# Four blocks of gated cross-attention and feed-forward layers: instruction order, the engine of two products and the queue of two transfers

## The chip, the cores and the metric

The kernel runs on one core of one Trainium2 chip. The metric is the time of one execution on the device in microseconds (us). The core has five engines, each of which works off its own instructions in order: TensorE (PE in the profile; its weight loads are PEld), VectorE (DVE), ScalarE (ACT), GpSimd (POOL) and SyncE (SP), which here only issues DMA transfers. An instruction that must wait for another engine or a transfer holds up everything behind it on its own engine.

## The reference

The input is x (32 sequences of 64 tokens, 256 features), a context of the same shape, and two gates of four numbers each. Eight layers follow one another, each of the form x = x + tanh(gate) * layer(layernorm(x), ...). The first three matter here:

```python
x = x + jnp.tanh(g_xattn[0]) * _L0_xattn_ref(32, 64, 256, w, u, _layernorm(x), ctx_2048)   # a decaying weighted mean along the sequence
x = x + jnp.tanh(g_ffn[0]) * _L0_ffn_ref(_layernorm(x), Wg, Wu, Wd, Wr, Ag, Bg, ...)       # experts
x = x + jnp.tanh(g_xattn[1]) * _L1_xattn_ref(_layernorm(x), ctx_2048)                      # convolution along the tokens
```

The first is a recurrence over the 64 tokens with running maxima, its keys being the normalised x and its values the context. In the second, every token is routed to the two best of eight experts. All experts share gate, up and down weights (704 hidden features) and differ by low-rank additions; for each of the two choices the hidden vector is silu(gate) * up. 704 is five times 128 and a remainder of 64. The third is a grouped convolution whose weights are the context. After them come a ternary-weight feed-forward layer, an 8-bit attention, a second ternary one, an attention with rotary positions, and a feed-forward layer with a Hadamard transform.

## The kernel before

The 2048 tokens lie in SBUF as 16 tiles of 128 tokens (c.x) for the whole run. The layers are Python generators, block0 to block7. The driver, program, interleaves them: it calls block1 step by step and, between its steps, as many steps of block0 as a formula allows; later in block1 it calls block2's first steps. Block 0 and block 1 go through the tokens in five chunks of 2, 2, 4, 4 and 4 tiles (CHUNKS), so that the first two chunks have 256 columns and the others 512.

The order in which the program is written is not the order in which an engine gets its instructions. Up to the end of block 3, a planner orders each engine's instructions by modelled times: what its model takes as ready early may go ahead of instructions written before it, and among those that are ready the earlier written one goes first. keep_in_program_order(ins) ties an instruction behind the one written last before it on its engine; it adds no wait for another engine.

The steps that the prediction speaks of:

- Layer norm. _mean (L107) takes a tile's statistics on VectorE (bn_stats, L110; bn_aggr, L113), and _inverse computes 1/sqrt(variance + eps) by a guess from the bits (L124, L92) and three Newton steps of three instructions (L96, L97, L98) on one to four numbers per partition. _stats does this for several tiles; with here=True it ties each bn_stats as above. _norm (L167) applies the result to a tile (xn), and _turned (L181) has TensorE transpose four tiles into PSUM (pt).
- Block 0 (L236 to L326). Per chunk, ScalarE copies the transposed, normalised x into kp (L317), VectorE runs a scan for the maxima (o, L270) and takes a difference (d, L271); exponentials on ScalarE, products on GpSimd, further scans and reciprocals on VectorE follow. w0s is prepared on VectorE at L255. The tanh of the eight gates (L326, in place in c.gate) is written after some steps of the first chunk.
- Block 1 (L333 to L558). head(i0, n) normalises and transposes a chunk (xf, L402 and L403), routes it (route, L363 to L390), spreads the routing over the ranks (ex on GpSimd L411, mt) and makes the low-rank inputs z (pz on TensorE L423, zg and zu on VectorE L426 and their sums on GpSimd L428). The chunk's body then does, for each 128 hidden features f, three gated steps (gated): shared weights alone (TensorE, L462), then the addition of one choice and of the other (L465). Each is followed by silu on ScalarE (sg, L468) and the product h on VectorE (L469), whose reading frees the PSUM bank. The three steps of an f are interleaved with those of the next ones (range(NF + 2)), 15 gated steps in all. The remainder of 64 features comes at the chunk's end (L484 to L501): both choices lie side by side in the partitions, gb and ub are copied from PSUM by ScalarE, and the two products ht[:, 1] = silu(gb) * ub (L491) and ht[:, 0] = silu(gs) * us (L501) are taken. TensorE then runs the down projections (pa L509 and L524, po L515, L532 and, at the next chunk's start, L537); zs is scaled on VectorE (L527, L529) and x updated (L542). The next chunk's head is run ahead, step by step, in the last third of a chunk.
- Block 2 (L565 to L663). Its weights, the context in another layout (c.wb, loaded at L1772 once block 0 has ended), come in two parts, and GpSimd adds their sum as a third part in four instructions of 512 columns (L593). window clears a padded buffer xw (L573). take(xw, q) normalises four tiles, q = 0 to 3, copies the transposed result into xw (L582 to L585) and adds a third part on GpSimd (L587). take 0 and take 1 are written during block 1's last chunk, after its gated steps 6, 8, 10 and 12; the convolution's matmuls (pc, L610) follow block 1.
- Transfers. SyncE issues, in this order, x and wu, the context of the first two chunks (ctx) and x of the second, the two gates (L1794, L1795), constants (con, L1796) and block 1's weights in two halves (wa, L1767 and L1768).

Of the kernel before, what the change touches and what calls it, by code (L numbers as in the profile page):

```python
# [22 lines left out]
ALU = mybir.AluOpType  # L23
# [3 lines left out]
P = 128  # L27
# [79 lines left out]
def _mean(c, pool, mv, i, here=False):  # L107

    st = pool.tile([P, 6], F32, tag="ln_st", name="ln_st", bufs=4)
    ins = c.nc.vector.bn_stats(st, c.x[:, i, :])  # L110
    if here:
        c.tc.keep_in_program_order(ins)
    c.nc.vector.bn_aggr(mv, st)  # L113


def _inverse(c, pool, mv, tag, bufs=1):

    return [r for r in _inverse_slowly(c, pool, mv, tag, bufs)][-1]
# [9 lines left out]
def _stats(c, pool, i0=0, n=NT, bufs=1, here=False):  # L128

    mv = pool.tile([P, max(n, 4), 2], F32, tag="ln_mv", name="ln_mv", bufs=bufs)[:, :n]  # L130
    for j in range(n):
        _mean(c, pool, mv[:, j, :], i0 + j, here)
    return mv, _inverse(c, pool, mv, "ln", bufs), i0
# [37 lines left out]
def _normT(c, pool, ps, ln, g, tag="ps"):  # L171

    return _turned(c, [_norm(c, pool, ln, 4 * g + q) for q in range(4)], ps, tag)
# [17 lines left out]
def _add_gatedT(c, src, hf, q, gate):  # L191

    _add_tilesT(c, src, hf, 4 * q, 4, gate)
# [138 lines left out]
def block1(c):  # L332
# [5 lines left out]
    nc = c.nc  # L338
# [11 lines left out]
    with ExitStack() as es:  # L350
        sm = es.enter_context(c.tc.tile_pool(name="sm1", bufs=1))
# [84 lines left out]
        for t, (i0, n) in enumerate(CHUNKS):  # L436
# [5 lines left out]
            def ahead():  # L442

                nonlocal step
                step += 1
                if nxt and step > STEPS - 8:
                    next(nxt, None)
# [3 lines left out]
            ht = hp.tile([P, 2, 512], F32, tag="ht", name="ht")[:, :, :N]  # L451
# [33 lines left out]
            gb, ub, gs, us = (full(hp, tag, tag) for tag in ("gb", "ub", "gs", "us"))  # L485
            sg = full(tp, "sg", "sg")
# [1 line left out]
                nc.scalar.copy(gb[s * S : (s + 1) * S], pg[:S])  # L488
                nc.scalar.copy(ub[s * S : (s + 1) * S], pg[S:])
            nc.scalar.activation(sg, gb, AF.Silu)  # L490
            nc.gpsimd.tensor_tensor(ht[:, 1, :], sg, ub, ALU.mult)  # L491
            ahead()
            yield
            pg, pu = full(ps, "ps", "pgs"), full(ps, "ps", "pus")
# [3 lines left out]
            nc.vector.tensor_tensor(gs, pg, gb, ALU.add)  # L498
            nc.scalar.activation(gs, gs, AF.Silu)
            nc.vector.tensor_tensor(us, pu, ub, ALU.add)  # L500
            nc.gpsimd.tensor_tensor(ht[:, 0, :], gs, us, ALU.mult)  # L501
            ahead()
            yield
            ahead()
# [52 lines left out]
def block2(c, begin):  # L557

    nc = c.nc
    w = c.wb[:, : 3 * LAGS * P].rearrange("p (k m g o) -> p k m g o", k=3, m=LAGS, g=2)  # L565
    Z = LAGS - 1
    with ExitStack() as es:
        sm = es.enter_context(c.tc.tile_pool(name="sm2", bufs=1, side="right"))

        def window(pool):  # L570

            xw = pool.tile([P, 3, 2, 16, Z + 32], F32, tag="xw", name="xw", bufs=1)
            nc.gpsimd.memset(xw.rearrange("p k h b s -> p (k h b) s")[:, :, 0:Z], 0.0)  # L573
            return xw

        def take(xw, q):

            ln = _stats(c, sm, 4 * q, 4)
            yield
            seqs = slice(8 * (q % 2), 8 * (q % 2) + 8)  # L580
            lo, hi = (pt.rearrange("p (b s r) -> p r b s", s=32, r=2) for pt in _normT(c, sm, c.aux, ln, q, "a"))
            nc.scalar.copy(xw[:, 0, 0, seqs, Z:], lo[:, 0])  # L582
            nc.vector.tensor_copy(xw[:, 1, 0, seqs, Z:], lo[:, 1])
            nc.scalar.copy(xw[:S, 0:2, 1, seqs, Z:], hi[S:])
            nc.vector.tensor_copy(xw[S:, 0:2, 1, seqs, Z:], hi[:S])  # L585
            for h in range(2):
                nc.gpsimd.tensor_tensor(xw[:, 2, h, seqs, Z:], xw[:, 0, h, seqs, Z:], xw[:, 1, h, seqs, Z:], ALU.add)  # L587
            yield

        n = LAGS * P // 4  # L590
        for j in range(4):
            at = [c.wb[:, (4 * k + j) * n : (4 * k + j + 1) * n] for k in range(3)]
            nc.gpsimd.tensor_tensor(at[2], at[0], at[1], ALU.add)  # L593
        xw = window(sm)
        for q in range(2):
            yield from take(xw, q)
        third = begin()
        tn = es.enter_context(c.tc.tile_pool(name="tn2", bufs=2, side="right"))
        ps = es.enter_context(c.tc.tile_pool(name="ps2", bufs=6, space=PSUM))
        fifths = weights5(c, tn)  # L600
        next(fifths)
        xws = [xw, window(tn)]
        casts, waiting, nth = [], [], 0

        def products(xw, k, pcs, lags):
            for m in lags:
                for h in range(2):
                    for a in range(2):
                        rows, to = slice(a * S, (a + 1) * S), slice((a ^ h) * S, ((a ^ h) + 1) * S)
                        nc.tensor.matmul(  # L610
                            pcs[h][to], w[rows, k, m, h, :], xw[rows, k, h, :, Z - m : Z - m + 32], start=m == 0, stop=m == Z
                        )

        def results(k, pcs, kept):

            for h in range(2):
                pv = pcs[h].rearrange("p (b s) -> p b s", s=32)
                if k == 1:
                    p1 = tn.tile([P, 16, 33], F32, tag=f"p1{h}", name=f"p1{h}", bufs=1)
                    yT = tn.tile([P, 1024], F32, tag=f"yT{h}", name=f"yT{h}", bufs=1)  # L620
                    nc.gpsimd.memset(p1[:, :, 0:1], 0.0)
                    nc.scalar.copy(p1[:, :, 1:], pv)
                    kept.append((p1, yT))
                    continue
                p1, yT = kept[h]
                to = yT.rearrange("p (b s r) -> p b s r", s=32, r=2)
                if k == 0:
                    nc.vector.tensor_tensor(to[:, :, :, 0], pv, p1[:, :, :32], ALU.add)
                    nc.vector.tensor_tensor(p1[:, :, 1:], pv, p1[:, :, 1:], ALU.add)
                else:  # L630
                    nc.vector.tensor_tensor(to[:, :, :, 1], pv, p1[:, :, 1:], ALU.subtract)

        slot = 0
        for n in range(2):
            kept = []
            for k in (1, 0, 2):
                pcs = [ps.tile([P, 512], F32, tag="ps", name="pc") for _ in range(2)]
                for part in range(2):

                    for z in casts:  # L640
                        ternary3(c, tn, *z)
                    casts = []
                    for _ in range((1 + (slot % 4 == 0)) if slot else 0):
                        if nth < 12:
                            casts.append(magnitudes3(c, tn, nth))
                            nth += 1
                    next(fifths, None)
                    products(xws[n], k, pcs, range(8 * part, 8 * part + 8))
                    for j in range(2):
                        if waiting:  # L650
                            yT, m, h, q = waiting.pop(0)
                            _add_gatedT(c, yT[:, q * 512 : (q + 1) * 512], h, 2 * m + q, c.gate[:, 1:2])
                    if part:
                        results(k, pcs, kept)
                    elif n == 0 and k in (1, 0):
                        for _ in take(xws[1], 3 - k):
                            pass
                    if slot == 9:
                        next(third)
                    slot += 1  # L660
            waiting = [(kept[h][1], n, h, q) for q in range(2) for h in range(2)]
        for z in casts:
            ternary3(c, tn, *z)  # L663
        for yT, m, h, q in waiting:
            _add_gatedT(c, yT[:, q * 512 : (q + 1) * 512], h, 2 * m + q, c.gate[:, 1:2])
    yield third
# [5 lines left out]
def magnitudes3(c, pool, n):  # L672

    wb = pool.tile([P, 512], BF16, tag="t_wb", name="t_wb", bufs=4)
    ab = pool.tile([P, 512], BF16, tag="t_ab", name="t_ab", bufs=4)
    c.nc.gpsimd.tensor_copy(wb, c.wa[:, n * 512 : (n + 1) * 512])
    c.nc.scalar.activation(ab, wb, AF.Abs)
    return n, wb, ab
# [1061 lines left out]
def program(tc, a, out):  # L1740
    nc = tc.nc
    with ExitStack() as es:
        one = es.enter_context(tc.tile_pool(name="one", bufs=1))
        c = SimpleNamespace(nc=nc, tc=tc)
# [42 lines left out]
        c.aux = es.enter_context(tc.tile_pool(name="aux", bufs=2, space=PSUM))  # L1787


        first, second = block0(c), block1(c)  # L1790
        next(first)
        early, conv_w = ExitStack(), ExitStack()
        c.wts = early.enter_context(tc.tile_pool(name="wts0", bufs=1))
        nc.sync.dma_start(c.gate[:, 0:4], a["g_xattn"].to_broadcast([P, 4]))  # L1794
        nc.sync.dma_start(c.gate[:, 4:8], a["g_ffn"].to_broadcast([P, 4]))  # L1795
        nc.sync.dma_start(c.con, a["con"])  # L1796
        load_wa("l0f", L0F_N)
        pieces, conv = 0, None
# [12 lines left out]
        with ExitStack() as w3s:  # L1811
            for k, _ in enumerate(second):
# [9 lines left out]
                at = k - STEPS * (len(CHUNKS) - 1)  # L1822
# [178 lines left out]
```

## Time and profile before

| | |
|---|---|
| median of 3 runs | 1333.27 us (1330.69 to 1333.59) |
| profiled execution | 1334.85 us, its span 1333.1 us |
| TensorE busy | 1199.2 us (90%) |
| VectorE, ScalarE, GpSimd busy | 905.1, 618.0, 456.1 us |
| 0 to 40 us: TensorE busy | 9.5 us |
| 40 to 365 us (block 1, with most of block 0): TensorE busy | 296.4 of 325 us |
| 365 to 560 us: TensorE busy | 183.4 of 195 us |

Three views of the profile are used. The page gives busy times and the chain of work that ended last, traced back from the last instruction. Busy time by stretches gives, for each stretch, its length, then busy time and instruction count of PE, PEld, DVE, ACT and POOL, then the clock granted to TensorE (1.00 is full speed), the busy share of the DMA engines and GB/s. The instructions in order of time give start, time, engine, line, operation, output and inputs and count; consecutive ones of a group are merged, so the time is that of the group, and the bracket at the end is the engine's idle time before it and what ended that. Times of operations with several entries in flight overlap a little.

### The profile page before, as it was taken

To read this page: it belongs to the slowest core of one execution; us is meant where nothing else is said; L and a number is where in the kernel's file an instruction comes from. 1 tells how busy PE (TensorE), PEld (TensorE's weight loads), DVE (VectorE), ACT (ScalarE), POOL (GpSimd) and SP (SyncE) were. 2 spreads that over 40 slices of the span, in tenths; PEclk is the share of its full clock that TensorE was granted. 3 is DMA by queue.
4 is the path that set the end of the run, shared out by engine and by line. 5 is a ranking of instruction groups with operands and counts; after the bars stand their busy time and mean duration, and the time that the engine had idled before them with its cause. 6 is when DMAs were issued, how large, how long until landed. Compare 5 with 4: busy or idle time off the path is not lost.

```text
span 1333.1 us, 21452 instructions
## 1 busy us (share of the span) xinstructions
PE 1199.2 (90%) x8342; PEld 724.3 (54%) x8342; DVE 905.1 (68%) x2195; ACT 618.0 (46%) x1046; POOL 456.1 (34%) x479
## 2 busy tenths in 40 slices
PE   0788899999999989988899976899999999999999
PEld 0666345454533367765666642455555555555665
DVE  6588867554348898768999996587787877532111
ACT  2553634322231145657899971455555555511100
POOL 3333606120123233335777775123225335000000
PEclk9899999989999999989999997799999999999999
DMA  6000000100052120000000010100000000000000
GB/s 216 21 1 16 0 0 1 63 1 0 8 213 97 33 103 1 1 0 2 2 2 2 2 64 1 60 37 1 2 2 1 2 2 1 1 8 8 16 16 16
DMA packets 10294, 34.14 MB, mean 26 GB/s; under 512 B 1360, under 2 KB 5968, under 8 KB 8528
## 3 DMA queue, kind: packets, MB, share of 16 engines
q1 hardware_dynamic: 10192, 32.76, 6.9%
q8 instruction: 66, 1.08, 0.4%
q14 instruction: 36, 0.29, 0.1%
HBM read 30.66 MB, written 2.10 MB: 25 GB/s over the span
## 4 chain that ended last, share of the span: by engine, by line
PE 56%; DVE 28%; POOL 5%; ACT 4%; issue 4%; DMA 2%; SPq 0%; DVEq 0%; POOLq 0%; ACTq 0%
PE pw L1563 6%; PE po L1586 5%; PE pp L1573 4%; PE po L1735 4%; PE pu L1725 4%; PE pg L1725 4%; PE pc L610 3%; PE pu L462 2%; PE pg L462 2%; PE pu L465 2%; PE pa L509 2%; PE po L515 2%; PE pg L465 2%; DVE xn L167 2%; DMA w<-in_l2f 1%
## 5 line engine op out<-in xcount | busy, mean ns | idle before, releaser
L1579 DVE TENSOR_REDUCE mx<-pp 128x4 f32<-128x1024 f32 x128 | 155.9, 1218 | 42.3 <-PE pp L1573 41.8
L1565 ACT ACTIVATE e<-pw 128x1024 f32<-128x1024 f32 x128 | 130.9, 1025 | 115.0 <-PE pw L1563 68.5
L1563 PE MATMUL pw<-qs,kb 32*128 32x256 f32 x1024 | 147.1, 408 | 7.5 <-DVE qs L1550 4.5
L1573 PE MATMUL pp<-kb,q 32*128 32x512 f32 x512 | 148.8, 665 | 4.8 <-POOL q L1534 4.0
L1563 PEld LDWEIGHTS pw<-qs,kb 32*128 32x128 f32 x1024 | 88.5, 187 | 52.3 <-issue 29.4
L468 ACT ACTIVATE sg<-pg 128x512 f32<-128x512 f32 (+1 forms) x75 | 37.8, 512 | 117.1 <-PE pg L462 51.6
L610 PE MATMUL pc<-xw,wb 64*64 64x512 f32 x768 | 90.0, 600 | 0.2 <-DVE x L542 0.2
L1728 DVE TENSOR_TENSOR h<-pu,sg 128x512 f32<-128x512 f32 x32 | 22.1, 692 | 80.8 <-PE pu L1725 80.8
L1727 ACT ACTIVATE sg<-pg 128x512 f32<-128x512 f32 x32 | 19.1, 597 | 122.8 <-PE pg L1725 122.7
L469 DVE TENSOR_TENSOR h<-pu,sg 128x512 f32<-128x512 f32 (+1 forms) x75 | 42.5, 573 | 49.1 <-PE pu L462 30.4
L1528 POOL TENSOR_TENSOR k<-t,t 128x512 f32<-128x512 f32 x16 | 20.3, 1268 | 148.4 <-DVE t L1513 148.4
L1586 PE MATMUL po<-e,va 128*32 128x256 f32 x1024 | 69.0, 387 | 1.8 <-ACT e L1565 1.8
L768 POOL TENSOR_TENSOR acc<-acc,sq 128x512 f32<-128x512 f32 x28 | 39.0, 1392 | 65.1 <-ACT sq L767 63.6
L1725 PE MATMUL pg<-xf,wa 128*128 128x512 f32 x128 | 60.3, 592 | 0.0
L1725 PE MATMUL pu<-xf,wa 128*128 128x512 f32 x128 | 60.3, 592 | 0.0
L610 PEld LDWEIGHTS pc<-xw,wb 64*64 64x64 f32 x768 | 29.9, 134 | 53.9 <-issue 53.2
L1735 PE MATMUL po<-hb,h 128*128 128x256 f32 x256 | 55.9, 379 | 0.0
L1735 PEld LDWEIGHTS po<-hb,h 128*128 128x128 f32 x256 | 48.6, 190 | 8.3 <-issue 1.9
L110 DVE BATCH_NORM_STATS2 ln_st<-x 128x6 f32<-128x256 f32 x112 | 44.1, 408 | 10.9 <-POOL x L1615 7.2
L1586 PEld LDWEIGHTS po<-e,va 128*32 128x32 f32 x1024 | 26.9, 109 | 44.3 <-issue 17.5
L1513 DVE SCALAR_TENSOR_TENSOR t<-pp,wb,con 128x512 f32<-128x512 f32 x64 | 45.0, 745 | 8.7 <-PE pp L1506 8.7
L1531 POOL TENSOR_SCALAR kb<-k,con 128x512 f32<-128x512 f32 x32 | 49.8, 1569 | 1.6
(342 smaller groups left out, 2946.8 us busy)
## 6 DMA issues: line engine op xcount, KB each, us to landing
w<-in_l2f SPq DMA_DIRECT2D x12, 512.0 KB, 3.9
wa<-in_l0f SPq DMA_DIRECT2D x2, 1828.0 KB, 13.0
wa<-in_l1f SPq DMA_DIRECT2D x2, 1536.0 KB, 9.4
wa<-in_l3f SPq DMA_DIRECT2D x2, 1536.0 KB, 8.0
wb<-in_conv SPq DMA_DIRECT2D x1, 2048.0 KB, 7.4
ctx<-in_ctxT SPq DMA_DIRECT2D x2, 1024.0 KB, 6.0
ctx<-in_ctxN SPq DMA_DIRECT2D x2, 1024.0 KB, 6.3
out<-x SPq DMA_DIRECT2D x16, 128.0 KB, 1.7
```

Of the source, the lines that this page charges most:

```text
L462: nc.tensor.matmul(p, wt[:, k, fc], xf[:, k, :N], start=k == 0, stop=False, skip_group_check=True)
L465: nc.tensor.matmul(p, wt[:, fc], z[m, s][:, :N], start=False, stop=s == 1, skip_group_check=True)
L610: nc.tensor.matmul(pcs[h][to], w[rows, k, m, h, :], xw[rows, k, h, :, Z - m : Z - m + 32], start=m == 0, stop=m == Z)
L1513: nc.vector.scalar_tensor_tensor(t[r], pp[:, :, r, :], bias[:, n, r : r + 1], f, ALU.add, ALU.mult)
L1531: nc.gpsimd.tensor_scalar(kb[:, :, h, :], k, odd[:, h : h + 1], None, ALU.mult)
L1563: nc.tensor.matmul(pw[:, jj, k, :], w.k[rows, h, k * P : (k + 1) * P], w.qs[rows, :], start=True, stop=True)
L1565: nc.scalar.activation(e, pw, AF.Exp, scale=scale)
L1573: nc.tensor.matmul(pp[:, jj], p.q[rows, t * P : (t + 1) * P], p.k[rows], start=True, stop=True)
L1579: nc.vector.tensor_reduce(p.mx[:, t, i0 : i0 + 2, 16:18], pp, AX.X, ALU.max, negate=True)
L1586: nc.tensor.matmul(po[strip(j), :], a.v[:, k, 2 * j + h, :], a.e[h, j][:, k, :], start=k == 0, stop=k == 1)
L1725: nc.tensor.matmul(p, wt[:, k, fc], xf[:, k, :], start=k == 0, stop=k == 1)
L1735: nc.tensor.matmul(po, h[:, f, q * P : (q + 1) * P], c.w2h[:, f, :], start=f == 0, stop=f == NH - 1)
```

## The change

It has three parts. The two products ht of the experts' last 64 features run on VectorE instead of GpSimd. In block 2 the four weight sums are kept in source order on GpSimd, and the eight bn_stats of take 0 and take 1 on VectorE. The two transfers of the gates are issued by ScalarE, and written ahead of block 0's first instructions instead of after them.

```diff
@@ -488,7 +488,7 @@
             nc.scalar.activation(sg, gb, AF.Silu)
-            nc.gpsimd.tensor_tensor(ht[:, 1, :], sg, ub, ALU.mult)
+            nc.vector.tensor_tensor(ht[:, 1, :], sg, ub, ALU.mult)
@@ -498,7 +498,7 @@
             nc.vector.tensor_tensor(us, pu, ub, ALU.add)
-            nc.gpsimd.tensor_tensor(ht[:, 0, :], gs, us, ALU.mult)
+            nc.vector.tensor_tensor(ht[:, 0, :], gs, us, ALU.mult)
@@ -575,7 +575,7 @@
         def take(xw, q):
 
-            ln = _stats(c, sm, 4 * q, 4)
+            ln = _stats(c, sm, 4 * q, 4, here=q < 2)
@@ -590,7 +590,7 @@
             at = [c.wb[:, (4 * k + j) * n : (4 * k + j + 1) * n] for k in range(3)]
-            nc.gpsimd.tensor_tensor(at[2], at[0], at[1], ALU.add)
+            c.tc.keep_in_program_order(nc.gpsimd.tensor_tensor(at[2], at[0], at[1], ALU.add))
@@ -1787,12 +1787,12 @@
+        nc.scalar.dma_start(c.gate[:, 0:4], a["g_xattn"].to_broadcast([P, 4]))
+        nc.scalar.dma_start(c.gate[:, 4:8], a["g_ffn"].to_broadcast([P, 4]))
         first, second = block0(c), block1(c)
         next(first)
         early, conv_w = ExitStack(), ExitStack()
         c.wts = early.enter_context(tc.tile_pool(name="wts0", bufs=1))
-        nc.sync.dma_start(c.gate[:, 0:4], a["g_xattn"].to_broadcast([P, 4]))
-        nc.sync.dma_start(c.gate[:, 4:8], a["g_ffn"].to_broadcast([P, 4]))
```

## The prediction

> **What bounds the kernel now.** I read the page first (busy shares, the chain that ended last), then the chain in order of time, then busy time by stretches of 5 us, and the instructions in order of time where TensorE was short.
>
> ```profile
> PE 1199.2 (90%) x8342; PEld 724.3 (54%) x8342; DVE 905.1 (68%) x2195; ACT 618.0 (46%) x1046; POOL 456.1 (34%) x479
> PE 56%; DVE 28%; POOL 5%; ACT 4%; issue 4%; DMA 2%; SPq 0%; DVEq 0%; POOLq 0%; ACTq 0%
> ```
>
> TensorE is busy for 90% and carries most of the chain, so time is won only where it stands idle or runs slowly. The edits touch blocks 0, 1 and the start of 2, the first 365 us. There the chain in order of time has one long transfer at the start:
>
> ```profile
> 4.59 6.58 DMA gate<-in_g_ffn
> ```
>
> It is read in the instructions of the first 12 us:
>
> ```profile
> 8.06 1.28 ACT L326 ACT_TABLE_LOAD   x1 [8.06 <-DMA gate<-in_g_xattn]
> ...
> 11.20 0.21 ACT L326 ACTIVATE gate<-gate 128x8 f32<-128x8 f32 x1 [1.85 <-DMA gate<-in_g_ffn]
> 11.31 0.63 ACT L317 COPY kp<-pt 128x256 f32<-128x256 f32 x2
> 11.77 1.29 DVE L270 TENSOR_TENSOR_SCAN o<-w,kp 128x260 f32<-128x260 f32 x2 [1.37 <-ACT kp L317]
> ```
>
> The tanh of the gates stands ahead of the copy of kp on ScalarE. TensorE's transposes for kp ended at 8.42, but the copy waited for a transfer that landed at 11.17, and VectorE's scan waited 1.37 us for the copy.
>
> The stretches around 265 us hold the largest loss of block 1's last three chunks:
>
> ```profile
> 260.00:265.00 5.00, 5.00 (x14) 1.61 (x12) 5.00 (x17) 2.26 (x4) 2.86 (x3) 1.00 0.24 102
> 265.00:270.00 5.00, 1.53 (x7) 1.06 (x7) 5.00 (x11) 1.29 (x4) 3.31 (x3) 0.75 0.00 0
> 270.00:275.00 5.00, 5.00 (x15) 2.13 (x13) 2.47 (x8) 2.98 (x4) 1.26 (x1) 0.57 0.01 2
> ```
>
> TensorE is busy 1.53 of 5 us while VectorE is full, and afterwards its clock is granted at 0.57. The cause, in order of time:
>
> ```profile
> 262.14 4.94 POOL L593 TENSOR_TENSOR wb<-wb 128x512 f32<-128x512 f32 x4 [6.13 <-DMA wb<-in_conv]
> 262.25 1.18 DVE L98 SCALAR_TENSOR_TENSOR ln_r<-ln_t,ln_r 128x4 f32<-128x4 f32 x1
> ...
> 267.05 1.26 POOL L491 TENSOR_TENSOR ht<-sg,ub 128x512 f32<-128x512 f32 x1
> 267.14 2.29 DVE L167 TENSOR_SCALAR xn<-x,ln_mv,ln_r 128x256 f32<-128x256 f32 x4
> 268.57 1.84 PEld L181 LDWEIGHTS pt<-ident,xn 128*128 128x128 f32 x8 [4.32 <-issue]
> 268.60 2.21 PE L181 MATMUL pt<-ident,xn 128*128 128x128 f32 x8 [3.47 <-DVE xn L167]
> ```
>
> The convolution's weight sums (L593) run on GpSimd 50 us before their place in the source, and meanwhile a VectorE instruction on four numbers per partition (L98) takes 1.18 us instead of 0.15: VectorE waits for GpSimd's running instruction. The same is seen at the end of the chunk before, from the products on GpSimd:
>
> ```profile
> 190.86 1.30 POOL L491 TENSOR_TENSOR ht<-sg,ub 128x512 f32<-128x512 f32 x1 [27.99 <-ACT sg L490]
> ...
> 191.06 1.12 DVE L98 SCALAR_TENSOR_TENSOR ln_r<-ln_t,ln_r 128x4 f32<-128x4 f32 x1
> 192.12 1.26 POOL L501 TENSOR_TENSOR ht<-gs,us 128x512 f32<-128x512 f32 x1
> 192.22 1.19 DVE L96 TENSOR_TENSOR ln_t<-ln_r 128x4 f32<-128x4 f32 x1
> ...
> 194.39 0.67 PE L181 MATMUL pt<-ident,xn 128*128 128x128 f32 x4 [2.03 <-DVE xn L167]
> ```
>
> **Gates on ScalarE's queue.** Both transfers become the first instructions on ScalarE, issued at about 0.7 to 1.6 us (two issues of 0.43 to 0.47 us, as they take on SyncE). ScalarE has nothing else until 8.06, which hides them. wu, of the same size, was issued at 1.22 and landed after 2.5 us; the gates took 3.9 and 6.6. Between these they land by 3 to 8.2, so table load and tanh are nearly or wholly over by 8.42 and kp is copied up to 2.8 us earlier. VectorE, however, works until 10.40 (the second L255, 9.92 + 0.48), so its scan moves from 11.77 to 10.40 at most: 1.37. The gates' small packets now run beside the first x, which VectorE awaits until 3.55; I allow 0.2 for that. Gain 1.2, bounds 0 (the gates land as late as now) and 2.8 (VectorE's order changes too). From here to TensorE's first large matmul at 34.67 every step is compute, so the gain goes through. On SyncE con and both halves of wa move up by the two issues, 0.95; wa is needed only at 34.08 and landed by 20, so that is worth nothing. The ctx loads behind them wait for GpSimd and move with it.
>
> [...]
>
> **Products on VectorE.** Ten instructions move: six of 128x512, 1.26 to 1.30 us on GpSimd, and four of 128x256, 0.73. VectorE's products of the same shapes take 0.69 (L500) and 0.41. Chunk by chunk:
> - Chunk 0: two of 0.41 enter a gapless VectorE chain (73 to 80 us) and nothing waited on GpSimd: +0.8, bounds 0 and 0.8.
> - Chunk 1: L98 took 0.58 and 0.59 beside GpSimd, 0.85 over its usual 0.16; two products of 0.41 take their place: 0.
> - Chunk 2: L98 and L96 above lost 0.96 and 1.03. Behind 190.88 the chain needs five short steps of 0.2 before xn. With both products ahead of it xn starts at 190.88 + 1.0 + 1.4 = 193.3, with none at 191.9, instead of 193.84. TensorE's wait of 2.03 shrinks by 0.5 to 1.9; I take 0.8. After that wait the clock was 0.66 (195 to 200), and pt, pa and pl took 1.01, 1.91 and 2.29 where 0.67, 1.02 and 1.85 are usual: 1.7 us. After a wait of 1.66 at 206.3 the clock stayed at 1.00, so a wait of 0.1 to 1.5 should keep it. Gain 2.5, bounds 0 and 3.6.
> - Chunk 4: VectorE is idle from 344, and the products are needed at 355.7: nothing.
>
> [...]
>
> **Weight sums and statistics in source order.** keep_in_program_order ties an instruction behind the one traced last on its engine. For L593 that is zu's sum of chunk 4 (L428, ends 292.53), so the four adds run from about 292.5 to 297.5. GpSimd is idle there until 324.9; the sums are first needed in block 2, after 365. The one VectorE instruction with two SBUF inputs there (L529 at 296.60) may wait 1.3 us, and its reader L537 runs at 304.29: hidden. For the eight statistics of take 0 and 1 it is VectorE's product after the sixth gated step of chunk 4, near 317 us. Out of 255 to 274 go eight L110 of 0.41, eight L113 of 0.17 and two chains of eleven at 0.16: 8.2 us of VectorE's work, and with L593 and L491 gone from GpSimd some 4 us of waiting (L98 1.03, L96 0.75, L97 and L98 together 1.3, xn 0.9). TensorE's wait was 3.47, so it should vanish: chunk 2's end carries as much VectorE work and two GpSimd products and waits 2.03. With it goes the slow clock: pt 2.21 instead of 1.04, pus 1.97 instead of 1.02, pa 1.93 instead of 1.02, 3.0 in all. Gain 6.5, bounds 3.5 and 6.5.
>
> Price: the 8.2 us land in 317 to 345. VectorE was busy 15.8 of the 25 us from 315 to 340 and nearly idle from 345 to 365, and xw is needed only at 365. Behind each statistic the h products L469 queue, whose results free TensorE's banks, and pt of take 0 (322.8) waits for xn in TensorE's order. I take 0.8, bounds 0 and 3.
>
> **Sum:** -1.2 + 0.8 - 2.5 - 6.5 + 0.8 = -8.6. The profiled execution took 1334.85 (span 1333.1), 1.6 above the median of the three runs, so 1326.3 for it and 1324.7 for a median: 1325. Nothing after 365 us runs to a fixed time, so the gain should stay.
>
> **Rivals.**
> - Slower: the statistics stall TensorE in chunk 4 as they did in chunk 3. VectorE then needs 15.8 + 8.2 = 24.0 of 25 us; if both transposes (322.8 and 332.6) come up before their xn, each costs as the one at 268.6 did, 3.47 + 3.0. That is 13 instead of 0.8, with the clock granted at half for longer, and the sum +3.6: 1337. It decides from two waits of about 2 us each. For it: the planner orders by modelled times, and misplaced work in chunk 3. Against: GpSimd is idle in chunk 4 but for L587, so VectorE is not held up, and TensorE's order has pa and po (342 to 361) to fill in. Chance 0.14.
> - Half: waiting in chunk 3 is only shortened to some 2 us and its clock still falls, and chunk 2 gains nothing: -1.2 + 0.8 + 0 - 1.5 + 0.8, about 1332, or no measurable change. Chance 0.13. The order is planned anew, so other waits can grow.
> - [...] Chance 0.15; it changes the size alone.
> - Forecast: 0.58.
>
> About 0.2%, 2.7 us, is what a measurement of this kernel can tell from no change. Forecast and late gates are faster, and a little of the half case; 0.76 faster, 0.10 same, 0.14 slower. The lower end takes the best bounds: 1333.3 - 2.8 - 3.6 - 6.5 = 1320, and 1 for other order; the upper end takes in the half case and the beginning of the slow one: 1319 to 1334.
>
> **What would show it.** Right: tanh before 8.4 us and the first scan near 10.4; no L593 before 290; no L110 for tiles 0 to 7 between 255 and 275; no wait over 1 us ahead of pt there and the clock at 1.00 from 265 to 275; at 190 us short VectorE steps of 0.2. Wrong: waits ahead of pt or behind L469 in chunk 4 with a lower clock, a GpSimd wait in its place, or later parts that stretch.

## The result, and the profile after

The changed kernel takes 1326.41 us (median of 6 runs, 1325.40 to 1327.52) against 1330.87 us for the kernel before (6 runs, 1328.67 to 1333.59): a ratio of 0.9969, with a 95% interval of 0.9957 to 0.9982. That is faster by 0.31%, or 4.5 us. A repetition, against the kernel before on the same chip, gave 0.9983 [0.9975, 0.9992]. The profiled execution after took 1327.04 us, its span 1325.3; the profiled one of before took 1334.85, which lies above all its six timed runs. So the two profiles differ by 7.8 us, where the medians differ by 4.5.

The busy times on the page of the changed kernel show the ten products that went from GpSimd to VectorE:

```profile
PE 1199.5 (91%) x8326; PEld 726.9 (55%) x8342; DVE 904.0 (68%) x2205; ACT 617.5 (47%) x1046; POOL 445.5 (34%) x469
```

VectorE has ten instructions more and yet is not busy for longer (905.1 us before): what it had lost beside GpSimd is at least what the products cost it, 6.00 us by its ten writes of ht. Up to 365 us the short steps L96 and L98 alone are busy for 13.4 us, against 19.3 in the profile before. The start of the changed kernel, in order of time:

```profile
4.17 0.75 DVE L110 BATCH_NORM_STATS2 ln_st<-x 128x6 f32<-128x256 f32 x2 [4.17 <-DMA x<-in_x]
5.21 1.28 ACT L326 ACT_TABLE_LOAD   x1 [5.21 <-DMA gate<-in_g_ffn]
6.50 0.21 ACT L326 ACTIVATE gate<-gate 128x8 f32<-128x8 f32 x1
...
8.80 0.80 ACT L317 COPY kp<-pt 128x256 f32<-128x256 f32 x2 [2.09 <-PE pt L181]
...
11.19 1.28 DVE L270 TENSOR_TENSOR_SCAN o<-w,kp 128x260 f32<-128x260 f32 x2
```

The tanh is done at 6.7 us instead of 11.4, and the copy of kp no longer waits for it. Yet the scan starts at 11.19 where 10.40 was hoped for: VectorE's first statistics wait for x until 4.17, and in the profile before, in order of time, until 3.55.

```profile
3.55 0.75 DVE L110 BATCH_NORM_STATS2 ln_st<-x 128x6 f32<-128x256 f32 x2 [3.55 <-DMA x<-in_x]
```

These are 0.62 of the 0.79 us. Most of the rest is wu, which VectorE takes up next (L252): it came 3.8 us after its issue instead of 2.5.

Busy time by stretches where the largest loss stood:

```profile
260.00:265.00 5.00, 5.00 (x32) 3.44 (x32) 1.95 (x8) 3.50 (x6) 0.00 (x0) 1.00 0.00 0
265.00:270.00 5.00, 5.00 (x16) 1.97 (x13) 4.86 (x17) 3.83 (x6) 1.01 (x1) 1.00 0.00 0
270.00:275.00 5.00, 5.00 (x23) 2.43 (x22) 0.48 (x1) 1.76 (x3) 1.84 (x3) 1.00 0.00 0
```

TensorE is busy throughout, at full clock; VectorE's column fell from 5.00 to 1.95 in the first stretch. The weight sums and the first of the pinned statistics now stand here in the order of time:

```profile
281.43 4.93 POOL L593 TENSOR_TENSOR wb<-wb 128x512 f32<-128x512 f32 x4
...
309.56 0.42 DVE L110 BATCH_NORM_STATS2 ln_st<-x 128x6 f32<-128x256 f32 x1
```

And the end of chunk 2, where the products now run on VectorE, in order of time:

```profile
190.86 4.56 PE L509 MATMUL pa<-h,wa 128*128 128x512 f32 x10
...
192.28 0.69 DVE L491 TENSOR_TENSOR ht<-sg,ub 128x512 f32<-128x512 f32 x1
192.88 0.15 DVE L98 SCALAR_TENSOR_TENSOR ln_r<-ln_t,ln_r 128x4 f32<-128x4 f32 x1
192.96 0.68 DVE L501 TENSOR_TENSOR ht<-gs,us 128x512 f32<-128x512 f32 x1
...
194.15 1.38 DVE L167 TENSOR_SCALAR xn<-x,ln_mv,ln_r 128x256 f32<-128x256 f32 x4
```

The short steps on four numbers take 0.15 each, not 1.12 to 1.19. TensorE has no wait left here: it was busy 5.00 of 5 us from 190 to 195, in the repeated profile of this kernel too.

### The profile page after: what moved, and what is told of

Same layout as the page of the kernel before. It is cut to its first block, busy times and chain, and to the rows that moved or that the text cites. A ratio compares the mean times of both kernels' runs of the same rounds, so it can differ in the third digit from the quotient of the medians.

```text
span 1325.3 us, 21428 instructions
## 1 busy us (share of the span) xinstructions
PE 1199.5 (91%) x8326; PEld 726.9 (55%) x8342; DVE 904.0 (68%) x2205; ACT 617.5 (47%) x1046; POOL 445.5 (34%) x469
## 4 chain that ended last, share of the span: by engine, by line
PE 59%; DVE 27%; ACT 4%; POOL 4%; issue 3%; DMA 2%; SPq 0%; DVEq 0%; POOLq 0%; ACTq 0%
PE pw L1563 6%; PE po L1586 5%; PE pp L1573 4%; PE po L1735 4%; PE pu L1725 4%; PE pg L1725 4%; PE pc L610 4%; PE pu L465 2%; PE pu L462 2%; PE pg L462 2%; PE pa L509 2%; PE po L515 2%; PE pg L465 2%; DVE xn L167 2%; DMA w<-in_l2f 1%
## 5 line engine op out<-in xcount | busy, mean ns | idle before, releaser
L610 PE MATMUL pc<-xw,wb 64*64 64x512 f32 x768 | 90.0, 600 | 0.2 <-DVE x L542 0.2
L469 DVE TENSOR_TENSOR h<-pu,sg 128x512 f32<-128x512 f32 (+1 forms) x75 | 42.4, 572 | 46.6 <-PE pu L462 32.2
L610 PEld LDWEIGHTS pc<-xw,wb 64*64 64x64 f32 x768 | 29.3, 134 | 53.5 <-issue 52.8
L110 DVE BATCH_NORM_STATS2 ln_st<-x 128x6 f32<-128x256 f32 x112 | 44.4, 408 | 11.6 <-POOL x L1615 7.2
```

Of the source, the lines that this page charges most:

```text
L610: nc.tensor.matmul(pcs[h][to], w[rows, k, m, h, :], xw[rows, k, h, :, Z - m : Z - m + 32], start=m == 0, stop=m == Z)
```

## The experiments

The kernels differ up to block 2 only, so the profiles are compared by when TensorE reaches fixed points: the first large matmul (L462), the start of each chunk's remainder (L484), and the first matmul of the convolution (L610), which is block 2's start. All times are starts in us. "Without" and "with" a part means that part of the change. The last column is the ratio to the kernel before, timed on the same chip.

| kernel | first L462 | L484, chunk 0 to 1 | chunk 1 to 2 | chunk 2 to 3 | chunk 3 to block 2 | block 2's start | ratio [95%] |
|---|---|---|---|---|---|---|---|
| before | 34.53 | 47.16 | 65.58 | 76.87 | 104.9 | 365.4 | |
| before, again | 33.24 | 47.15 | 65.56 | 76.87 | 104.8 | 363.5 | 0.9991 [0.9979, 1.0003] |
| gates alone | 34.64 | 47.78 | 65.56 | 75.30 | 104.2 | 362.8 | 1.0007 [0.9997, 1.0018] |
| products alone | 33.67 | 52.04 | 64.55 | 73.44 | 101.5 | 360.4 | 0.9998 [0.9986, 1.0011] |
| order alone | 33.78 | 47.14 | 65.57 | 76.87 | 99.2 | 357.9 | 0.9956 [0.9940, 0.9972] |
| sums alone | 35.01 | 47.71 | 65.59 | 75.31 | 98.5 | 357.6 | one run |
| statistics alone | 34.47 | 47.72 | 65.57 | 75.30 | 99.8 | 358.3 | one run |
| after | 33.89 | 50.34 | 64.52 | 73.44 | 98.4 | 356.8 | 0.9969 [0.9957, 0.9982] |
| after, again | 34.35 | 52.03 | 64.52 | 73.43 | 98.3 | 357.2 | 0.9983 [0.9975, 0.9992] |
| order, wide products | 35.13 | 47.13 | 65.58 | 73.43 | 98.3 | 355.4 | 0.9952 [0.9934, 0.9969] |
| the same, again | 34.67 | 47.13 | 65.54 | 73.45 | 98.4 | 355.4 | 0.9953 [0.9940, 0.9965] |
| the same, gates too | 34.68 | 47.82 | 65.56 | 73.45 | 98.4 | 355.2 | 0.9947 [0.9931, 0.9964] |
| order, wide products, tanh held | 35.24 | 47.16 | 65.59 | 73.43 | 98.4 | 355.8 | 0.9966 [0.9953, 0.9979] |

The column "chunk 3 to block 2" holds the order's gain, "chunk 0 to 1" a loss of the products, and "chunk 2 to 3" their gain.

**The kernel before, again.** No edit.

> The kernel before once more, to see how far one execution differs from another where the instructions are the same. Theory: the losses read from the first profile are the kernel's own. Block 2's first matmul (L610) then starts at 365.4 within 1 us, the wait of 3.47 us at 265 us and the lower clock after it are there again, and any difference in time comes after 365 us. Rival: the first profile was an unlucky execution; block 2 then starts by 3 us or more earlier, because the clock does not fall after 265 or after 192 us.

Its span was 1327.3, 5.8 us shorter than in the first profile, of which 1.9 by block 2's start. Its waits, in order of time on TensorE, are nearly those of the first profile:

```profile
192.56 0.67 PE L181 MATMUL pt<-ident,xn 128*128 128x128 f32 x4 [2.03 <-DVE xn L167]
...
265.92 0.45 PE L181 MATMUL pt<-ident,xn 128*128 128x128 f32 x1 [2.62 <-DVE xn L167]
```

So the waits belong to the program, but this execution was shorter than the first profiled one. A comparison of one profile with one profile is off by this much.

**The gates alone.**

```diff
+        nc.scalar.dma_start(c.gate[:, 0:4], a["g_xattn"].to_broadcast([P, 4]))
+        nc.scalar.dma_start(c.gate[:, 4:8], a["g_ffn"].to_broadcast([P, 4]))
         first, second = block0(c), block1(c)
...
-        nc.sync.dma_start(c.gate[:, 0:4], a["g_xattn"].to_broadcast([P, 4]))
-        nc.sync.dma_start(c.gate[:, 4:8], a["g_ffn"].to_broadcast([P, 4]))
```

> The kernel before with the gates' transfers alone changed. Theory (the parts add, and the first x lands later beside the gates' packets): the first VectorE scan starts about 0.6 us earlier than the 11.77 of before, block 2 starts at 364.8, and the wait of 3.5 us at 265 us stays; the time is 0.6 us shorter, less than can be measured. Rival (the gates count in full, as predicted): block 2 starts 1.2 us earlier. [...]

1331.49 us, 1.0007: nothing gained. The tanh started at 6.46, but the scan at 11.92 and the first large matmul at 34.64, as late as before (11.77 and 34.53). Block 2 starts 2.6 us earlier all the same (362.8 against 365.4). Of these, 1.6 come from the clock: the wait of 2.03 us at the end of chunk 2 is there, but this time the clock stayed at 1.00 behind it (75.30 against 76.87).

**The products alone.**

```diff
-            nc.gpsimd.tensor_tensor(ht[:, 1, :], sg, ub, ALU.mult)
+            nc.vector.tensor_tensor(ht[:, 1, :], sg, ub, ALU.mult)
...
-            nc.gpsimd.tensor_tensor(ht[:, 0, :], gs, us, ALU.mult)
+            nc.vector.tensor_tensor(ht[:, 0, :], gs, us, ALU.mult)
```

> The kernel before with the products of the experts' last 64 on VectorE alone. Theory: the wait of 2.03 us at 192 us goes and the clock stays at 1.00 from 195 to 200, which is worth 2.5 to 3.7 us; the wait at 265 us stays, since L593 still runs there, and may shrink by 0.9. Block 2 starts at 361.5 to 363. Rival: the clock falls all the same and only the wait shrinks, 364.5. Rival: the products hold VectorE up in chunk 0 and 1 by as much as they win, 365.4.

1331.01 us, 0.9998. The wait at the end of chunk 2 is gone, as in the changed kernel, and the chunk is 3.4 us shorter than in the kernel before, but chunk 1 became 4.9 us longer (52.04 against 47.15). Block 2 starts at 360.4, earlier than expected and 3.1 us earlier than in the repeated profile of the kernel before, and yet the total shows no gain.

**The order alone.**

```diff
-            ln = _stats(c, sm, 4 * q, 4)
+            ln = _stats(c, sm, 4 * q, 4, here=q < 2)
...
-            nc.gpsimd.tensor_tensor(at[2], at[0], at[1], ALU.add)
+            c.tc.keep_in_program_order(nc.gpsimd.tensor_tensor(at[2], at[0], at[1], ALU.add))
```

> The kernel before with the weight sums and the eight statistics alone kept in source order. Theory: the wait of 3.47 us at 265 us and the lower clock behind it go, 5.5 to 6.5 us; the wait at 192 us stays, since the products still run on GpSimd; chunk 4 costs under 1 us. Block 2 starts at 359 to 360. Rival: GpSimd's product L491 alone still delays xn by about 1 us and TensorE waits 1 to 2 us with the clock falling, block 2 at 362. Rival: the statistics stall chunk 4 and block 2 starts at 364 or later.

1326.06 us, 0.9956 [0.9940, 0.9972]: the whole gain of the change, by this part. From chunk 3's remainder to block 2 it takes 99.2 us against 104.8 for the kernel before, again: 5.6 less. The longest wait left there, in order of time on TensorE, is this one:

```profile
272.87 0.66 PE L415 MATMUL pm<-ident,ex 128*128 128x128 f32 x4 [0.76 <-POOL ex L411]
```

GpSimd ran the two products (L491 and L501, 269.77 to 272.26) between its first copy of ex (L411) and its second, for which pm waits.

**The weight sums alone, and the statistics alone.** Each half of that diff by itself.

> The kernel before with the four weight sums alone kept in source order; the eight statistics stay early. Theory (GpSimd's instruction held VectorE up): without it the short steps ahead of xn take 0.16 instead of up to 1.2 us, xn comes about 3 us earlier, TensorE's wait at 265 us falls from 2.5 to 3.5 to under 1 us and block 2 starts 3 to 6 us earlier than the 363.5 of the repeated run. Rival (VectorE's 8.2 us of early statistics are the cause): the wait stays above 2 us and block 2 starts at 362 or later.

> The kernel before with the eight statistics alone kept in source order; the weight sums still run at about 262 us. Theory (the two causes add, either alone is nearly enough): the head of chunk 4 has its xn by about 261, before the sums begin, and the wait ahead of its transposes is under 1 us; block 2 starts at 358 to 360. Rival (the sums hold VectorE up whatever it does): short VectorE steps of about 1 us stand ahead of xn, the wait is 2 us or more and block 2 starts at 361 or later.

One run each: 1325.81 and 1328.59, with 1330.53 as the median of before on that chip. Either half takes the wait at 265 us away, and 98.5 and 99.8 us pass from chunk 3's remainder to block 2. So VectorE was late only by both together, the statistics' work and the waiting beside GpSimd's sums. With the statistics alone TensorE waits a little later for GpSimd, 1.40 us ahead of pm at 273.31. This is not the sums' doing, which ended at 265.4: again the products stand between two copies of ex (270.21 to 272.71). The run with the sums alone also holds the counterpart of the wait at the end of chunk 2, in order of time:

```profile
189.66 2.84 PE L509 MATMUL pa<-h,wa 128*128 128x512 f32 x6
...
194.53 0.67 PE L181 MATMUL pt<-ident,xn 128*128 128x128 f32 x4 [2.03 <-DVE xn L167]
```

It is as long as that of the kernel before. The two stretches that follow it differ, though; first the kernel before, again, then the sums alone:

```profile
195.00:200.00 5.00, 5.00 (x23) 3.24 (x23) 3.59 (x7) 1.10 (x3) 0.00 (x0) 0.78 0.00 0
```

```profile
195.00:200.00 5.00, 5.00 (x29) 3.51 (x28) 3.42 (x7) 1.07 (x2) 0.00 (x0) 1.00 0.00 0
```

The clock fell after the wait in one execution (0.78) and not in the other (1.00). This is the difference between 76.87 and 75.30 in the table's column "chunk 2 to 3".

**Order and wide products.** The products on VectorE only in the chunks of 512 columns; the gates on SyncE as before.

```diff
-            nc.gpsimd.tensor_tensor(ht[:, 1, :], sg, ub, ALU.mult)
+            (nc.vector if n == 4 else nc.gpsimd).tensor_tensor(ht[:, 1, :], sg, ub, ALU.mult)
...
-            nc.gpsimd.tensor_tensor(ht[:, 0, :], gs, us, ALU.mult)
+            (nc.vector if n == 4 else nc.gpsimd).tensor_tensor(ht[:, 0, :], gs, us, ALU.mult)
```

> Sums and statistics in source order, the products on VectorE for the chunks of four tiles only, the gates as before. Theory (the products win in chunks 2 and 3 and lose in chunk 1, where the planner's order changes): from the end of chunk 0 to that of chunk 1 it takes 47.1 us as before (after: 50.3), the wait at 192 us is gone, and block 2 starts 3 to 5 us earlier than the 357.9 with order alone; the time is 1322. Rival (the clock after each wait is chance and the products themselves win nothing): block 2 within 1 us of 357.9, time 1326.

1324.76 us, 0.9952. Chunk 1 takes 47.13 us again, and chunk 2 keeps its gain (73.43). Block 2 starts 2.5 us earlier than with the order alone (355.4 against 357.9), but the totals do not tell the two apart (0.9952 and 0.9956).

**The same, with the tanh held at its place.** If the late gates only hurt because ScalarE takes the tanh ahead of the copy of kp, tying the tanh to its place should be worth more than a new queue.

```diff
-                    nc.scalar.activation(c.gate, c.gate, AF.Tanh)
+                    c.tc.keep_in_program_order(nc.scalar.activation(c.gate, c.gate, AF.Tanh))
```

> As the one before it, and the tanh of the gates kept in source order behind the first copies of kp, with the gates' transfers on SyncE as before. Theory (the gates' early transfers delay the first x by 0.6 us, and waiting for late gates costs 0 to 1.3 us, so that the order of the tanh is the better remedy): the first x is there at 3.5, the first scan starts at 10.4 in every execution and TensorE's first large matmul at 33.1, 0.1 to 1.4 us before those of the runs without it. Rival: the tanh or a second table load then stands in the way of the exponentials, and the first large matmul comes at 34 or later.

1325.90 us, 0.9966: a miss. With the tanh out of the way the scan started at 12.37, as in the wide variant before it (12.37). VectorE's order is another one here: ahead of the scan it now has a cast that waits for a transfer, and behind that the last steps of the second tile pair's layer norm with its xn, together 1.2 us. In order of time:

```profile
10.99 0.23 DVE L1821 CAST pairsb<-con 128x128 bf16<-128x128 f32 x1 [0.34 <-DMA con<-in_con]
...
11.72 0.73 DVE L167 TENSOR_SCALAR xn<-x,ln_mv,ln_r 128x256 f32<-128x256 f32 x2
12.37 1.28 DVE L270 TENSOR_TENSOR_SCAN o<-w,kp 128x260 f32<-128x260 f32 x2
```

**The change again, and the wide products with the gates on each queue.** Three kernels on one chip.

> The changed kernel once more, for a second profile. Theory (chunk 1's new order comes from the narrow products and is fixed in the program): the time between the remainders of chunk 0 and chunk 1 is again about 50.3 us, against 47.1 without those products, TensorE idles at 100 to 105 us again, and the clock after it may differ. Rival (that stretch was a chance of one execution): 47 to 48 us. Time 1326 by both, within 1.5.

> The change with the products on VectorE only in the three chunks of 512 columns; gates on ScalarE's queue. Theory (narrow products cost 3.2 us in chunk 1): 47.1 us between the remainders of chunks 0 and 1, and a time 2 to 3 us under the changed kernel on the same chip, 1323.5. If the gates' transfers cost what their delay of the first x suggests (0.6 us), it is 0 to 1 us above the same kernel with the gates on SyncE. Rival (the stretch is made up for later, by a clock that falls at another place): the same as the changed kernel within 1 us.

> Order and wide products, the gates on SyncE as before: the kernel that was fastest so far, beside the two above on one chip. Theory (narrow products cost 3.2 us, the gates' queue nothing or a loss of up to 0.6): 1323 to 1324.5, 2 to 3 us under the changed kernel. Rival (the gates' queue gains the 1.2 us that was forecast): about 1 us slower than the kernel with wide products and the gates on ScalarE's queue.

The change gave 1327.36 us (0.9983), wide products with the gates on ScalarE's queue 1324.05 (0.9947), and with the gates on SyncE 1322.95 (0.9953). Neither interval of the wide ones touches that of the change, [0.9975, 0.9992]: giving the narrow products back to GpSimd is worth 3.3 us with the gates alike, and both wide versions beat the change and the kernel before. The two wide ones are not told apart. Their starts show why; first with the gates on ScalarE's queue, then on SyncE:

```profile
4.17 0.75 DVE L110 BATCH_NORM_STATS2 ln_st<-x 128x6 f32<-128x256 f32 x2 [4.17 <-DMA x<-in_x]
...
9.00 0.75 DVE L110 BATCH_NORM_STATS2 ln_st<-x 128x6 f32<-128x256 f32 x2 [0.91 <-DMA x<-in_x]
...
11.95 1.28 DVE L270 TENSOR_TENSOR_SCAN o<-w,kp 128x260 f32<-128x260 f32 x2
```

```profile
3.53 0.75 DVE L110 BATCH_NORM_STATS2 ln_st<-x 128x6 f32<-128x256 f32 x2 [3.53 <-DMA x<-in_x]
...
11.36 0.21 ACT L326 ACTIVATE gate<-gate 128x8 f32<-128x8 f32 x1 [0.21 <-DMA gate<-in_g_ffn]
...
11.94 1.29 DVE L270 TENSOR_TENSOR_SCAN o<-w,kp 128x260 f32<-128x260 f32 x2 [1.54 <-ACT kp L317]
```

The scan waits 1.54 us for the late tanh in the second, and not at all in the first; but there VectorE itself is late, by 0.64 at the first statistics and by 0.91 more at the second tile pair. Both scans start at 11.95.

## Why the prediction was right, and where its steps were not

The predicted time was 1325, measured 1326.41, within the range and faster as forecast. In the first two profiles block 2 starts 8.6 us earlier (365.4 and 356.8), which is the sum forecast, to the tenth. That is luck: its errors cancelled, and both executions were drawn from a spread of some microseconds. By the table that gain is made of 0.6 up to the first large matmul, 0.1 up to chunk 0's remainder, -2.1 for chunks 0 to 2, 3.4 up to chunk 3's remainder and 6.5 from there.

| term | forecast | measured | by which comparison |
|---|---|---|---|
| gates | -1.2 | 0 | scans at 11.95 and 11.94, otherwise equal kernels |
| products, chunks 0 and 1 | +0.8 | +2.1 to +3.8 | L484 of chunk 0 to that of chunk 2: 114.86 (after), 116.55 (again), 112.74 (before) |
| products, chunk 2 | -2.5 | -3.4 or -1.9 | 73.43 against 76.87 or 75.30 |
| order, with its price in chunk 4 | -5.7 | -5.6 | 99.2 against 104.8, chunk 3 to block 2 |
| products, end of chunk 3 | not counted apart | -0.9 | 98.3 against 99.2, with the order in both |

**Order: right in mechanism, and in size where the clock had fallen.** The wait ahead of pt is gone and the clock stays at 1.00 from 260 to 275. The 3.0 us that the prediction counted for the slow clock hang on the execution: with the products alone TensorE waited 2.55 us ahead of pt (266.00), the clock stayed at 1.00 from 260 to 275, and from chunk 3's remainder to block 2 it took 101.5 us, only 3.1 more than with the change. Of the price of 0.8 in chunk 4 next to nothing was paid: TensorE was busy for 44.92 us of the 45 from 275 to 320 and for 44.80 of those from 320 to 365, and in the kernel before, again, for 45.00 and 44.80. The rival by which the statistics would stall TensorE there is thereby refuted. The 0.9 us that the products win at the end of chunk 3 are for the most part the wait of 0.76 for ex, which the prediction had not seen. The place was off for L593: it ran at 281.43, not from 292.5. The sum that it is tied behind (L428 of zu) had itself moved up to 280.21; nobody waited for it there. VectorE's L529, which by the prediction might wait 1.3 us beside the sums, came behind them, at 287.25, and took 0.69. Beside the sums in the profile before, L96 and L98 took up to 1.18 us instead of 0.15, while L110 (0.41) and L469 (0.68) took no longer than elsewhere; beside the product L491, four xn (L167) took 2.29 instead of 1.38.

**Gates: the term failed at the allowance of 0.2 for the transfers.** The step that the tanh would be over before the copy of kp was right. But in all four profiles with the gates on ScalarE's queue the first statistics waited until 4.11 to 4.17, and in the nine others until 3.34 to 3.72: the new packets cost the first x 0.6 us, and the second x, in three of the four, 0.56 to 0.91 more (in one of the nine others it was late too, by 1.36). VectorE, not the copy, then sets the scan's start. Nor was the 1.37 to be won a fixed amount: in the eight profiles with the late gates and the tanh left free, the scan waited 0 to 1.92 us for kp. In the prediction the chance of 0.15 stood for a gates' term of nothing, and nothing is what it came to; yet the gates do not land late, they land about 5 to 6.5 us earlier, and it is x that lands later. No run shows in what way the gates' packets delay it. Over these profiles the scan starts at 11.7 on average with the gates moved (four) and at 11.6 without (eight, the tanh left free), and the first large matmul lies at 33.89 to 34.68 and at 33.24 to 35.13: the spread of one program is larger than the effect.

**Products, chunks 0 and 1: the mis-sized term.** Its upper bound of 0.8 counted only VectorE's own work and took the planner's order as fixed. With the narrow products on VectorE the planner ordered chunk 1 anew: of the eight matmuls of pz (L423), four now stand ahead of a gated pair (L462, 93.33) that stood ahead of all eight before (92.07), and the gated matmuls behind them have changed places. TensorE's waits there in the changed kernel, in order of time, and then those of the kernel before:

```profile
98.63 0.70 PE L465 MATMUL pu<-zu,wa 128*128 128x256 f32 x2 [1.26 <-DVE h L469]
...
102.39 1.76 PE L465 MATMUL pg<-zg,wa 128*128 128x256 f32 x4 [2.19 <-ACT sg L468]
105.41 2.07 PE L465 MATMUL pu<-zu,wa 128*128 128x256 f32 x4 [1.27 <-DVE h L469]
...
111.14 1.13 PE L462 MATMUL pu<-xf,wa 128*128 128x256 f32 x4 [1.95 <-DVE h L469]
```

```profile
103.14 1.62 PE L465 MATMUL pg<-zg,wa 128*128 128x256 f32 x4 [3.26 <-ACT sg L468]
...
108.99 0.70 PE L465 MATMUL pu<-zu,wa 128*128 128x256 f32 x2 [0.86 <-DVE h L469]
```

Four waits of 6.67 us stand against two of 4.12. The products h queue on VectorE behind a scan and reciprocals of block 0 (L287, 2.2 us; L299, 1.7 each), and TensorE now meets these at a point where it has less other work. How much that costs hangs on the clock, too: from 110 to 115 us it was 1.00 in the first profile of the change and 0.66 in the second, where chunk 1 took 1.7 us longer. The wide variant, which leaves chunks 0 and 1 alone, has 47.13 us again, so the cause is the two narrow pairs. Which of these order changes weighs most was not tried.

**Products, chunk 2: right, with help that was not forecast.** The wait of 2.03 became none, but the short steps account for half of it. From TensorE's first pa (L509) to the first xn it takes 3.29 us (190.86 to 194.15), against 4.32 in the profile before (189.52 to 193.84): 1.03 less. The rest is TensorE's new order, which the prediction took as fixed: ten matmuls of pa stand ahead of the transposes, and six stood there before, so that 1.7 us more of work cover the remaining wait. Its worth hangs on whether the clock would have fallen: 1.9 us without that, 3.4 with it. The 1.7 that the prediction counted for the clock is paid in some executions only: of the six profiles that have this wait, three paid it (before, before again, order alone) and three did not (gates, sums, statistics alone).

**The base.** The prediction put the profiled execution 1.6 above the median of three runs. It lay 4 above the median of six, and further runs of the kernel before had medians of 1330.34 (29 runs) and 1329.19 (17). A gain of 8.6 against a long execution is one of 6.3 to 6.7 against the repeated profile (363.5 to 357.2 and 356.8).

**What stays open.** Of these 6.5 us the totals show 1.8 to 4.5. From within block 2 on, the kernels give each engine the same instructions in the same order, but from block 2's start to the end it took from 963.8 us (before, again) over 966.0 and 968.5 (the change, twice) to 970.6 (order, wide products). It took 967.7 both in the first profile of the kernel before, where block 2 starts last, and in that of the wide products with the gates moved, where it starts first. From 580 to 640 us, for instance, the granted clock was 0.91 in the profile before and 0.77 in that after. No run tells whether this is chance alone or hangs on when block 2 starts.

## What to carry to other kernels

An instruction of no urgency that a planner has moved forward can cost more than its own time when it fills an engine just before others need it: with the early statistics left where they were, tying down the weight sums, 4.9 us of GpSimd, shortened the way from chunk 3's remainder to block 2 by 6.3 us (104.8 to 98.5, one run). Here two ties to the source order gave all that this change gained, and either alone, in one run each, nearly sufficed. An edit that moves work between engines is to be priced with the planner's new order in mind, chunk by chunk, and kept only where a wait is seen: the same edit won 2 to 3 us of TensorE's time in chunk 2 and lost 2 to 4 in chunk 1. Before summing against a profiled execution, see how far it lies from the median of many runs.

## What was not expected of the hardware

After the same wait of 2.03 us (2.02 in one execution), at the same place, the granted clock from 195 to 200 us was 0.66, 0.78 and 0.80 in three executions and 1.00 in three others. No run shows what decides between the two.

Eight numbers per partition, issued on a second queue beside the first loads, delayed by 0.6 us a load that was needed before them (4.11 to 4.17 against 3.34 to 3.72).
